# Selective scan on one core: the product with C as one GpSimd instruction for three channel tiles, last columns by DMA, and the diagonal form of B for every state

## The chip, the core and the metric

The kernel runs on one core of one Trainium2 chip. The time is the device time of one launch in microseconds (us). The kernel before was timed in three runs; their median counts. The profile is one execution recorded by the hardware profiler. Its engines are TensorE (PE; its weight loads are listed apart as PEld), VectorE (DVE), ScalarE (ACT), GpSimd (POOL), and SyncE (SP), which here issues most DMA transfers.

## The reference, cut to what matters

The program is a chain of four layers on an image of 8 x 64 x 64 positions and 192 channels. The second layer holds a selective scan over 384 channels, in four directions over the 4096 positions, with 16 states for each channel. Cut down, it computes:

```python
# B = 8 images, K = 4 directions, Din = 384 channels, N = 16 states, L = 4096 positions
x_dbl = einsum('bkdl,kcd->bkcl', xs, x_proj_weight)
dts, Bs, Cs = split(x_dbl, [12, 12 + 16], axis=2)
dts = einsum('bkrl,kdr->bkdl', dts, dt_projs_weight)
A = -exp(A_logs).reshape(4, Din, N)
delta = softplus(dts + dt_projs_bias[None, :, :, None])
for l in range(L):                      # lax.scan
    dA  = exp(delta[l][..., None] * A)
    dBu = delta[l][..., None] * Bs[l][:, :, None, :] * xs[l][..., None]
    h   = dA * h + dBu
    y[l] = sum(h * Cs[l][:, :, None, :], axis=-1)
out_y = y + xs * Ds
```

All arithmetic is in fp32. The layers before and after (a state-space block with convolutions and an MLP, a depthwise convolution with layer norm and projection, two depthwise convolutions) are the same in both kernels.

## The kernel before

`layer1_scan` does the scan. The positions are cut into pieces of 512 (`NJ`), so there are 8 images x 4 directions x 8 pieces = 256 entries in `steps`; a *step* is one of them. Within a step the work runs over the 16 states (`N1`) and, for each state, over the three channel tiles of 128 (`DT`): 48 iterations. A *group* `g` is one state of one step, that is three iterations; `j` counts iterations over the whole stage, 12,288 in all. An engine executes its instructions in the order in which the program issues them, because the scan is built inside `every_engine`, which fixes the order of PE, DVE, ACT and POOL. SP's order is the scheduler's.

Iteration `j` of the main loop does, in this order:

- At the first tile of a group, `fetch(g + 2)` asks SP for a transfer of the row of C for that state, broadcast to 128 partitions (`bc`, 128 x 512, line 993).
- `ahead(j + 2)` makes the two inputs of the recurrence two iterations early. ACT computes the decay `dA` = exp(delta x A) (line 1003). PE forms delta x B x u in a PSUM bank `pd` (three banks), in four blocks of 128 x 128. The tile `dut` holds delta x u with positions on partitions, so PE has to turn it and to scale it by B. For even states (`diagonal(g)`) it does both in one true matmul: `dut` is the weight and `bd` is a diagonal matrix that holds B (line 1009). For odd states ACT has scaled `dut` by B beforehand (`sb`, 128 x 384) and PE only transposes it with the identity (line 1011).
- `scale(g + 2, ...)` lets ACT make those factors two groups early, four per group: `bd` from the identity (128 x 128) or `sb` from `dut` (128 x 384), both at line 987.
- `scan(j)` is the recurrence on DVE, one `tensor_tensor_scan` over 512 positions (line 1044). It writes tile `o` of `h` (128 x 3 x 512, two buffers). POOL multiplies that tile with `bc` into `hc` (six buffers, line 1053). After the third tile POOL copies the last column of each tile to `st`, the start of the same state in the next piece (line 1055).
- `behind(j - 2)` adds the 16 states: PE transposes `hc` in four blocks and accumulates them in the PSUM bank `yt` of that channel tile (`add_rows`, line 942).

Once per step a second sequence from `prepare` is threaded between these instructions. It loads the rows of the next piece (`xt`, `dut`), turns them (line 888), makes delta (PE at line 901, three ACT passes at lines 906 to 912, DVE at line 915), turns delta (line 922) and multiplies it into `dut` (DVE, line 928). `take` copies the finished `yt` out (ACT, line 957), and the copy goes to DRAM. In one of four directions, four blocks per tile with a diagonal of D are added to `yt` (also line 942, tile `dD`).

Of the kernel before, what the change touches and what calls it, by code (L numbers as in the profile page):

```python
# [10 lines left out]
AF = mybir.ActivationFunctionType  # L11
ALU = mybir.AluOpType
# [6 lines left out]
DIN = 384  # L19
DP, DT = 128, 3  # L20
NH, HD, NS = 6, 64, 64
N1, R1, K1 = 16, 12, 4
# [3 lines left out]
NJ = 512  # L26
# [3 lines left out]
class Names:  # L30
    n = 0


def mk(pool, shape, tag, **kw):
    Names.n += 1
    return pool.tile(shape, F32, tag=tag, name=f"{tag}_{Names.n}", **kw)
# [46 lines left out]
def every_engine(tc):  # L83
    ET = mybir.EngineType
    return tc.manual_schedule(engines={ET.PE, ET.DVE, ET.Activation, ET.Pool})
# [586 lines left out]
def layers123(ctx: ExitStack, tc, a, dr, x1, mv1, out, cst):  # L672
# [31 lines left out]
    yk = [[mk(dr, [L, DIN], f"y{b}_{k}") for k in range(K1)] for b in range(B)]  # L704
    layer1_in(tc, a, load, w_in, normed, ur, ut, xd, cst)
    layer1_scan(tc, a, load, ur, ut, xd, yk, cst)
    x2 = [mk(dr, [CP, CT, L], f"x2d{b}") for b in range(B)]
    x3 = [mk(dr, [CP, CT, L], f"x3d{b}") for b in range(B)]
# [123 lines left out]
def layer1_scan(ctx: ExitStack, tc, a, load, ur, ut, xd, yk, cst):  # L832

    nc = tc.nc
    ident = cst[0]
# [15 lines left out]
    sp = ctx.enter_context(tc.tile_pool(name="s1", bufs=2))  # L851
# [87 lines left out]
    def add_rows(yt, src, mat, first, last):  # L939

        for t in range(NB):
            nc.tensor.matmul(  # L942
                yt[:, t * 128 : (t + 1) * 128],
                src[:, t * 128 : (t + 1) * 128],
                mat,
                is_transpose=mat is ident,
                start=first and t == 0,
                stop=last,
                skip_group_check=True,
            )  # L950
# [16 lines left out]


    PER = N1 * DT
    total = len(steps) * PER  # L970
    ready = [{} for _ in steps]
    brows, decay, turned, states, held, outs, sts = {}, {}, {}, {}, {}, {}, {}

    def diagonal(g):
        return g % 2 == 0

    def scale(g, ts):
        if g >= len(steps) * N1:
            return
        m, n = ready[g // N1], g % N1  # L980
        for t in ts:
            if diagonal(g):
                v, src = mk(sp, [128, 128], "bd", bufs=10), ident
            else:
                v, src = mk(sp, [128, DIN], "sb", bufs=8), m["dut"][:, t, :]
            brows[g, t] = v
            nc.scalar.activation(v, src, AF.Copy, scale=m["xt"][:, t, 1 + R1 + n : 2 + R1 + n])  # L987

    def fetch(g):
        if g < len(steps) * N1:  # L990
            bc = held[g] = mk(sp, [128, NJ], "bc", bufs=4)
            n = g % N1
            nc.sync.dma_start(bc, ready[g // N1]["bcd"][n : n + 1, :].to_broadcast((128, NJ)))

    def ahead(j):

        if not 0 <= j < total:
            return
        g, o = divmod(j, DT)
        s, n = divmod(g, N1)  # L1000
        k = steps[s][1]
        dA = decay[j] = mk(sp, [DP, NJ], "dA", bufs=5)
        nc.scalar.activation(dA, ready[s]["dl"][:, o, :], AF.Exp, scale=aneg[:, k, o, n : n + 1])  # L1003
        pd = turned[j] = mk(pb, [128, NJ], "pd")
        cols = slice(o * 128, (o + 1) * 128)
        for t in range(NB):
            dst = pd[:, t * 128 : (t + 1) * 128]
            if diagonal(g):
                nc.tensor.matmul(dst, ready[s]["dut"][:, t, cols], brows[g, t], start=True, stop=True)  # L1009
            else:  # L1010
                nc.tensor.transpose(dst, brows[g, t][:, cols], ident)  # L1011

    def behind(j):
        if not 0 <= j < total:
            return
        g, o = divmod(j, DT)
        s, n = divmod(g, N1)
        b, k, p, _ = steps[s]
        if n == 0:
            outs[s, o] = mk(py, [128, NJ], "yt", bufs=DT)  # L1020
        add_rows(outs[s, o], states.pop(j), ident, n == 0, n == N1 - 1)
        if k == 0 and n == 8:
            add_rows(outs[s, o], ready[s]["u", o], dD[:, o, :], False, False)
        if n == N1 - 1:
            late.append((take, s, o, outs.pop((s, o))))

    def scan(j):
        if not 0 <= j < total:
            return
        g, o = divmod(j, DT)  # L1030
        s, n = divmod(g, N1)
        b, k, p, first = steps[s]
        if k == 0 and n == 5:
            v = ready[s]["u", o] = mk(sp, [DP, NJ], "uD", bufs=DT)
            nc.sync.dma_start(v, ur[b][:, o, p * NJ : (p + 1) * NJ])
        if first and n == 0 and o == 0:
            sts[k] = mk(pp, [DP, DT, N1], "st")
        st = sts[k]
        rev = slice(None, None, -1) if k >= 2 else slice(None)
        last = 0 if k >= 2 else NJ - 1  # L1040
        if o == 0:
            states["h"] = mk(sp, [DP, DT, NJ], "h", bufs=2)
        h = states["h"]
        nc.vector.tensor_tensor_scan(  # L1044
            h[:, o, rev],
            decay.pop(j)[:, rev],
            turned.pop(j)[:, rev],
            0.0 if first else st[:, o, n : n + 1],
            ALU.mult,
            ALU.add,  # L1050
        )
        hc = states[j] = mk(sp, [DP, NJ], "hc", bufs=6)
        nc.gpsimd.tensor_tensor(hc, h[:, o, :], held[g], ALU.mult)  # L1053
        if o == DT - 1:
            nc.gpsimd.tensor_copy(st[:, :, n], h[:, :, last])  # L1055

    with every_engine(tc):
        for _, f, *v in prepare(*steps[0][:3], ready[0]):
            f(*v)
            if f.__name__ == "turned_xd":  # L1060
                tc.keep_in_program_order(nc.scalar.preload_act_table_set("natural_log_exp_and_others"))
        fetch(0)
        fetch(1)
        scale(0, range(NB))
        scale(1, range(NB))
        ahead(0)
        ahead(1)
        todo, late = [], []
        for j in range(total + 3):
            g, o = divmod(j, DT)  # L1070
            s, i = divmod(j, PER)
            if i == 5 and s + 1 < len(steps):
                todo = prepare(*steps[s + 1][:3], ready[s + 1])
            if o == 0:
                fetch(g + 2)
            ahead(j + 2)
            scale(g + 2, ((0, 1), (2,), (3,))[o])
            while late:
                f, *v = late.pop(0)
                f(*v)  # L1080
            scan(j)
            behind(j - 2)
            while todo and todo[0][0] <= i - 5:
                _, f, *v = todo.pop(0)
                f(*v)
# [367 lines left out]
```

## Time and profile before

| | |
|---|---|
| Three runs | 25,094.24, 25,105.1 and 25,116.98 us; median 25,105.1 us |
| Profiled execution | span of 25,098.0 us from the first to the last instruction; the page lists no time around it |
| Busy share of the span | PE 95%, weight loads 74%, DVE 89%, ACT 80%, POOL 70% |
| The scan in the trace | about 6,680 to 22,890 us (first and last product with `bc`), 12,288 products at 1289 ns |
| Scan on DVE | 10,752 at 1262 ns with a start state, 1,536 at 1204 ns without |
| ACT's factors of B | 8,192 `bd` at 395 ns, 8,192 `sb` at 609 ns |
| PE's records | fp32 matmuls leave two records each, transposes one; line 1009: 49,152, line 1011: 24,576, line 942: 49,152 |
| Copies of last columns | 4,096 on POOL at 201 ns |

The page gives the busy time of an engine and, for each group of equal instructions, the count, the busy time and the mean duration of one. Durations on PE include the drain of the pipeline, so they overlap: the distance between starts, not the duration, is what PE's records cost one after the other.

### The profile page before, as it was taken

The numbers are of one execution on the slowest core, as the hardware profiler recorded it, in microseconds if no ns is written. First come the engines' busy times: TensorE is split into PE (matmuls) and PEld (weight loads), VectorE is DVE, ScalarE is ACT, GpSimd is POOL, SyncE is SP. The second block draws the span as 40 slices with busy tenths as digits, with TensorE's granted clock in tenths as the row PEclk, the third lists the DMA queues.
The fourth block names the chain that finished last, engine by engine and source line by source line (L and its number), as shares of the span: only waits on it lengthen the run. The fifth ranks groups of instructions, "written<-read, shape, count | busy, mean of one in ns | idle before, by whom it ended". The sixth has DMA issues, their size and how long they took to land.

```text
span 25098.0 us, 445961 instructions
## 1 busy us (share of the span) xinstructions
PE 23784.2 (95%) x156672; PEld 18458.1 (74%) x156672; DVE 22334.3 (89%) x26682; ACT 20190.7 (80%) x40488; POOL 17651.1 (70%) x18332
## 2 busy tenths in 40 slices
PE   8999999988899999999999999999999999998999
PEld 4444444445688888888888888888888888885333
DVE  6777777766799999999999999999999999998887
ACT  4555555544599999999999999999999999997443
POOL 2322322310399999999999999999999999995110
PEclk8888888899999999999999999999999999999999
DMA  1111111123333333333333333333333333335554
GB/s 59 47 43 46 46 47 43 38 70 114 110 100 95 96 101 95 95 103 95 95 101 97 95 99 98 95 97 100 95 95 104 95 95 102 95 95 157 170 175 122
DMA packets 1506272, 2337.12 MB, mean 93 GB/s; under 512 B 249997, under 2 KB 775949, under 8 KB 1504026
## 3 DMA queue, kind: packets, MB, share of 16 engines
q1 hardware_dynamic: 1496858, 2283.42, 31.5%
q8 instruction: 1236, 20.25, 0.3%
q0 software_dynamic: 7168, 25.17, 0.3%
q14 instruction: 1010, 8.27, 0.1%
HBM read 1847.54 MB, written 460.59 MB: 92 GB/s over the span
## 4 chain that ended last, share of the span: by engine, by line
PE 36%; ACT 31%; DVE 13%; POOL 13%; issue 6%; DMA 0%; POOLq 0%; SPq 0%; DVEq 0%; ACTq 0%
ACT dA L1003 13%; POOL hc L1053 11%; ACT sb L987 7%; PE pd L1009 6%; PE yt L942 5%; DVE h L1044 5%; ACT bd L987 4%; PE cv L1282 4%; PE y L592 3%; PE pd L1011 2%; PE mm L901 2%; PE fc L626 2%; PE y L519 1%; PE cv L774 1%; PE tp L564 1%
## 5 line engine op out<-in xcount | busy, mean ns | idle before, releaser
L1053 POOL TENSOR_TENSOR hc<-h,bc 128x512 f32<-128x512 f32 x12288 | 15431.9, 1289 | 475.6 <-DVE h L1044 341.2
L1044 DVE TENSOR_TENSOR_SCAN h<-dA,st,pd 128x512 f32<-128x512 f32 x10752 | 12949.5, 1262 | 530.1 <-PE pd L1009 374.4
L1003 ACT ACTIVATE dA<-dl,A_logs 128x512 f32<-128x512 f32 x12288 | 8817.1, 718 | 47.0 <-DVE h L1044 39.6
L942 PE MATMUL yt<-sq,hc 128*128 128x128 f32 x49152 | 7489.3, 275 | 200.1 <-POOL hc L1053 93.8
L1009 PE MATMUL pd<-bd,dut 128*128 128x128 f32 x49152 | 6581.4, 277 | 254.4 <-DVE h L1044 232.1
L1009 PEld LDWEIGHTS pd<-bd,dut 128*128 128x128 f32 x49152 | 5968.5, 192 | 609.9 <-PE yt L942 342.9
L942 PEld LDWEIGHTS yt<-sq,hc 128*128 128x128 f32 x49152 | 5669.7, 141 | 644.3 <-POOL hc L1053 624.4
L987 ACT ACTIVATE sb<-dut,xt 128x384 f32<-128x384 f32 x8192 | 4779.5, 609 | 1.1 <-DVE dut L928 1.0
L1011 PE MATMUL pd<-sq,sb 128*128 128x128 f32 x24576 | 3739.5, 275 | 8.5 <-DVE h L1044 0.4
L1011 PEld LDWEIGHTS pd<-sq,sb 128*128 128x128 f32 x24576 | 2823.6, 141 | 479.1 <-DVE dl L915 380.8
L987 ACT ACTIVATE bd<-sq,xt 128x128 f32<-128x128 f32 x8192 | 3026.3, 395 | 0.0
L1044 DVE TENSOR_TENSOR_SCAN h<-dA,pd 128x512 f32<-128x512 f32 x1536 | 1770.8, 1204 | 117.0 <-PE pd L1009 67.2
L1143 POOL TENSOR_TENSOR yin<-yin,yin 128x1536 f32<-128x1536 f32 x64 | 233.9, 3655 | 1635.1 <-DMA yin<-y 892.5
L1282 PE MATMUL cv<-x,dgi 96*96 96x512 f32 (+1 forms) x2560 | 1175.0, 595 | 9.3 <-ACT x L1271 9.1
L481 POOL TENSOR_TENSOR xdt<-xb,dtv 128x384 f32<-128x384 f32 x256 | 217.1, 848 | 1186.6 <-ACT xb L475 1186.6
L234 DVE SCALAR_TENSOR_TENSOR x<-xs,cpe_w,x 96x504 f32<-96x504 f32 (+1 forms) x1024 | 886.6, 866 | 31.8 <-ACT x L222 21.7
L784 DVE SCALAR_TENSOR_TENSOR u<-xa,conv_w,u 128x504 f32<-128x504 f32 x1152 | 850.1, 743 | 50.5 <-ACT u L776 12.5
L1282 PEld LDWEIGHTS cv<-x,dgi 96*96 96x96 f32 x2560 | 413.0, 164 | 638.2 <-issue 604.5
L901 PE MATMUL mm<-xs,w_dt 13*128 13x512 f32 x1536 | 863.0, 641 | 1.8 <-DVE dl L915 1.0
L1055 POOL COPY st<-h 128x3 f32<-128x3 f32 x4096 | 825.0, 201 | 0.0
L1303 DVE SCALAR_TENSOR_TENSOR y<-x,wi,y 96x504 f32<-96x504 f32 x1024 | 796.0, 796 | 17.7
L626 PE MATMUL fc<-ff,fc_w 128*96 128x512 f32 x1536 | 791.0, 621 | 2.7 <-DVE xo L629 2.7
(263 smaller groups left out, 26186.7 us busy)
## 6 DMA issues: line engine op xcount, KB each, us to landing
bc<-bcd SPq DMA_DIRECT2D x4096, 256.0 KB
yin<-y SPq DMA_DIRECT2D x256, 768.0 KB
csb<-csd SPq DMA_DIRECT2D x256, 384.0 KB
dut<-ut SPq DMA_DIRECT2D x128, 768.0 KB
y<-ys SPq DMA_DIRECT2D x128, 768.0 KB
dut<-ut SPq DMA_DIRECT2D x256, 384.0 KB
y<-ys SPq DMA_DIRECT2D x256, 384.0 KB
xt<-x1d SPq DMA_DIRECT2D x128, 384.0 KB
```

The source lines that it names most:

```text
L234: nc.vector.scalar_tensor_tensor(d[:, :, w0:w1], s[:, dy : dy + R, w0 + dx : w1 + dx], w[:, ct, tap : tap + 1], d[:, :, w0:w1], ALU.mult, ...
L626: nc.tensor.matmul(ps, f2w[:, o, ct * CP : (ct + 1) * CP], ff[:, o, :], start=o == 0, stop=o == 5)
L784: nc.vector.scalar_tensor_tensor(uv[:, o, :, w0:w1], tv[:, o, dy : dy + R, w0 + dx : w1 + dx], cw[:, o, tap : tap + 1], uv[:, o, :, w0:w1] ...
L901: nc.tensor.matmul(ps, w_dt[:, k, o * 128 : (o + 1) * 128], made["xs"][0 : 1 + R1, :], start=True, stop=True)
L942: nc.tensor.matmul(yt[:, t * 128 : (t + 1) * 128], src[:, t * 128 : (t + 1) * 128], mat, is_transpose=mat is ident, start=first and t == 0 ...
L987: nc.scalar.activation(v, src, AF.Copy, scale=m["xt"][:, t, 1 + R1 + n : 2 + R1 + n])
L1003: nc.scalar.activation(dA, ready[s]["dl"][:, o, :], AF.Exp, scale=aneg[:, k, o, n : n + 1])
L1009: nc.tensor.matmul(dst, ready[s]["dut"][:, t, cols], brows[g, t], start=True, stop=True)
L1011: nc.tensor.transpose(dst, brows[g, t][:, cols], ident)
L1044: nc.vector.tensor_tensor_scan(h[:, o, rev], decay.pop(j)[:, rev], turned.pop(j)[:, rev], 0.0 if first else st[:, o, n : n + 1], ALU.mult, ...
L1053: nc.gpsimd.tensor_tensor(hc, h[:, o, :], held[g], ALU.mult)
L1282: nc.tensor.matmul(pv[:, :, w0:w1], dgi[:, ct, j, :], sv[:, dy : dy + R, w0 + dx : w1 + dx], start=j == 0, stop=j == len(TAPS) - 1, skip_g ...
```

## The change

The change has three parts. (1) The product with C is made once per group, for all three channel tiles, by one POOL instruction on 128 x 1536 elements, with `bc` repeated over the tiles by a step of zero. `hc` becomes a tile of 128 x 3 x 512 with three buffers, `h` gets three buffers in place of two, and `behind` runs six iterations after the scan (`LAG`) in place of two. (2) The copy of the last columns from `h` to `st` is taken from POOL; SP issues it as a DMA of 128 x 3 single elements, ahead of the product. (3) Every state uses the diagonal form: ACT makes four `bd` per group (14 buffers), and PE four true matmuls per iteration. `sb` and the transposes of line 1011 are gone. Line numbers after the first edited one are 6 to 7 lower in the changed kernel.

```diff
     PER = N1 * DT
+    LAG = 2 * DT
...
-    def diagonal(g):
-        return g % 2 == 0
-
     def scale(g, ts):
...
         for t in ts:
-            if diagonal(g):
-                v, src = mk(sp, [128, 128], "bd", bufs=10), ident
-            else:
-                v, src = mk(sp, [128, DIN], "sb", bufs=8), m["dut"][:, t, :]
-            brows[g, t] = v
-            nc.scalar.activation(v, src, AF.Copy, scale=m["xt"][:, t, 1 + R1 + n : 2 + R1 + n])
+            v = brows[g, t] = mk(sp, [128, 128], "bd", bufs=14)
+            nc.scalar.activation(v, ident, AF.Copy, scale=m["xt"][:, t, 1 + R1 + n : 2 + R1 + n])
...
-            if diagonal(g):
-                nc.tensor.matmul(dst, ready[s]["dut"][:, t, cols], brows[g, t], start=True, stop=True)
-            else:
-                nc.tensor.transpose(dst, brows[g, t][:, cols], ident)
+            nc.tensor.matmul(dst, ready[s]["dut"][:, t, cols], brows[g, t], start=True, stop=True)
...
-        add_rows(outs[s, o], states.pop(j), ident, n == 0, n == N1 - 1)
+        add_rows(outs[s, o], states[g][:, o, :], ident, n == 0, n == N1 - 1)
+        if o == DT - 1:
+            del states[g]
...
-            states["h"] = mk(sp, [DP, DT, NJ], "h", bufs=2)
+            states["h"] = mk(sp, [DP, DT, NJ], "h", bufs=3)
...
-        hc = states[j] = mk(sp, [DP, NJ], "hc", bufs=6)
-        nc.gpsimd.tensor_tensor(hc, h[:, o, :], held[g], ALU.mult)
         if o == DT - 1:
-            nc.gpsimd.tensor_copy(st[:, :, n], h[:, :, last])
+            nc.sync.dma_start(st[:, :, n], h[:, :, last])
+            hc = states[g] = mk(sp, [DP, DT, NJ], "hc", bufs=3)
+            nc.gpsimd.tensor_tensor(hc, h, held.pop(g).unsqueeze(1).to_broadcast((DP, DT, NJ)), ALU.mult)
...
-        for j in range(total + 3):
+        for j in range(total + LAG + 1):
...
-            behind(j - 2)
+            behind(j - LAG)
```

## The prediction

> **What bounds the kernel now.** I read the slices of the page first, then one stretch inside the scan by engine, then that stretch's groups by line, then PE's order of time. The scan is the stage from 6,680 to 22,890 us; nothing else is edited. I take 8,000 to 20,000 us as its sample. This is the stretch; the columns after the 12,000 us are the busy times of PE, PEld, DVE, ACT and POOL, then the granted clock, the DMA share and GB/s.
>
> ```profile
> ...
> 8000.00:20000.00 12000.00, 11660.32 (x96277) 10626.90 (x96276) 11486.90 (x10422) 11720.86 (x23686) 11707.76 (x12127) 1.00 0.35 98
> ...
> ```
>
> Four engines seem full: PE 97%, ACT 98%, POOL 98%, DVE 96%. For PE this is not its true load, because its records overlap. The groups of the same stretch (count, busy time, mean ns, idle before) give what each engine does:
>
> ```profile
> ...
> L1053 POOL TENSOR_TENSOR hc<-h,bc 128x512 f32<-128x512 f32 x9096 | 11422.1, 1289 | 292.3 <-DVE h L1044 192.5 <-PE yt L942 29.2 <-issue 1.7
> L1044 DVE TENSOR_TENSOR_SCAN h<-dA,st,pd 128x512 f32<-128x512 f32 x7945 | 9568.5, 1262 | 392.1 <-PE pd L1009 276.8 <-PE pd L1011 58.9 <-ACT sb L987 22.6
> ...
> L942 PE MATMUL yt<-sq,hc 128*128 128x128 f32 x36385 | 5543.5, 275 | 145.1 <-POOL hc L1053 66.8
> L1009 PE MATMUL pd<-bd,dut 128*128 128x128 f32 x36384 | 4871.7, 277 | 188.6 <-DVE h L1044 172.1
> ...
> L987 ACT ACTIVATE sb<-dut,xt 128x384 f32<-128x384 f32 x6064 | 3537.5, 609 | 0.0
> L1011 PE MATMUL pd<-sq,sb 128*128 128x128 f32 x18192 | 2768.1, 275 | 5.9
> L987 ACT ACTIVATE bd<-sq,xt 128x128 f32<-128x128 f32 x6065 | 2240.5, 395 | 0.0
> ...
> L901 PE MATMUL mm<-xs,w_dt 13*128 13x512 f32 x1134 | 635.3, 640 | 0.0
> ...
> L922 PE MATMUL mm<-sq,dl 128*128 128x128 f32 x2274 | 372.1, 273 | 0.0
> ...
> L942 PE MATMUL yt<-dD,uD 128*128 128x128 f32 x1152 | 152.2, 275 | 0.0
> ...
> L888 PE MATMUL mm<-sq,xt 128*45 128x128 f32 x756 | 113.4, 273 | 0.0
> ...
> ```
>
> Each step has 192 records of the sum over states (48 iterations, four blocks), so 36,385 records are 189.5 steps and a step lasts 12,000 / 189.5 = 63.32 us. What PE's records cost back to back stands in PEld's order of time (start, length, what, count):
>
> ```profile
> ...
> 10002.00 0.47 PEld L942 LDWEIGHTS yt<-sq,hc 128*128 128x128 f32 x4
> 10002.44 0.47 PEld L1011 LDWEIGHTS pd<-sq,sb 128*128 128x128 f32 x4
> 10002.88 0.47 PEld L942 LDWEIGHTS yt<-sq,hc 128*128 128x128 f32 x4
> 10003.32 0.47 PEld L1011 LDWEIGHTS pd<-sq,sb 128*128 128x128 f32 x4
> 10003.75 0.47 PEld L942 LDWEIGHTS yt<-sq,hc 128*128 128x128 f32 x4
> 10004.39 0.29 PEld L901 LDWEIGHTS mm<-xs,w_dt 13*128 13x128 f32 x2 [0.17 <-issue]
> 10005.44 0.42 PEld L1011 LDWEIGHTS pd<-sq,sb 128*128 128x128 f32 x4 [0.76 <-DVE dl L915]
> 10005.83 0.47 PEld L942 LDWEIGHTS yt<-sq,hc 128*128 128x128 f32 x4
> 10006.26 0.97 PEld L1009 LDWEIGHTS pd<-bd,dut 128*128 128x128 f32 x8
> 10007.15 0.47 PEld L942 LDWEIGHTS yt<-sq,hc 128*128 128x128 f32 x4
> 10007.59 0.97 PEld L1009 LDWEIGHTS pd<-bd,dut 128*128 128x128 f32 x8
> 10008.48 0.47 PEld L942 LDWEIGHTS yt<-sq,hc 128*128 128x128 f32 x4
> 10008.92 0.97 PEld L1009 LDWEIGHTS pd<-bd,dut 128*128 128x128 f32 x8
> ...
> ```
>
> Read the starts. From 10002.00 to 10003.75 sixteen transposes follow each other: 1.75 / 16 = 0.1094 us each. From 10006.26 to 10008.92 lie sixteen records of true matmuls and eight transposes: (2.66 - 8 x 0.1094) / 16 = 0.1116 us each. A block of four costs 0.44 us as transposes and 0.89 us as matmuls, since an fp32 matmul leaves two records. Nothing is waited for in these runs, so this is PE's pace. The two records of line 901 cost 10005.44 - 10004.19 = 1.25 us, less 0.05 that the next four regain: 1.20.
>
> PE's need in the stretch is then 57,607 transposes (36,385 + 18,192 + 2,274 + 756) x 0.1094 = 6,302 us; 36,384 + 1,152 records of line 1009 and of D x 0.1116 = 4,189; 567 pairs of line 901 x 1.20 = 680. The sum is 11,171 us, 93.1%, or 58.95 us per step. Only 4.4 us per step are free. The other engines by busy time: POOL 61.8, ACT 61.9, DVE 60.6 us per step. DVE's own pace is longer than its busy time says: its order of time has four scans in 4.88 us, so 48 x 1.22 + 3 x 0.67 (line 915) + 4 x 0.53 (line 928) = 62.7 us. POOL, ACT and DVE set the pace together, and PE is 4 us behind them.
>
> **The change part by part.**
>
> *Product with C.* Three products of 1289 ns and a copy of 201 ns per group go; one product of 128 x 1536 comes. The nearest row is the tail's sum of two dense tiles of this size on POOL (line 1143), 3655 ns mean. Three separate products, 3867 ns, are the upper bound for a fused one, unless the step of zero in `bc` is slow, for which no row speaks. I take 3.66 us: POOL needs 16 x 3.66 = 58.5 us per step in place of 61.8. The gain is real but only POOL's.
>
> *Diagonal form on ACT.* The chain of waits runs along ACT here and shows starts 0.505 us apart for `sb`, 0.29 for `bd`. 32 of 64 factors per step change: 32 x 0.215 = 6.9 us less, ACT falls from 61.9 to about 55 us.
>
> *Diagonal form on PE.* Half of the blocks of `pd` turn from transposes into matmuls. In the stretch, 18,192 records at 0.1094 (1,990 us) become 36,384 at 0.1116 (4,060 us): 2,070 us more, 10.92 us per step. PE then needs 58.95 + 10.92 = 69.87 us per step. This is 7 us above the next engine, and above today's 63.32. It lies on the path, because the 4.4 us of cover that exist are used up first: 6.55 us per step come through.
>
> The Trainium skill ("TensorE: Matmul & The Clock Gate", section "Back-to-back issue gap") gives about 81 ns for a weight load with a matmul of 128 columns in a sustained stream. By an estimate from that figure the 598 records of 128 columns per step would cost 48 us, 52 with line 901, PE would stay under DVE, and the change would bring time. The trace has 109 to 112 ns here at a granted clock of 1.00, and the measurement decides.
>
> *Clock.* The stretch is granted 1.00 with PE at 93%, and the fully packed runs above have the same, so I price a denser PE at the same clock.
>
> *Last columns by DMA.* SP issues 16 more transfers per step, each waiting for a group's third scan. An issue takes 0.32 us (`bc`) to 0.60 us (`xt`, four rows per partition), so 5 to 10 us of SP's 69.9. Behind it in SP's queue stands the fetch of `bc` for three groups later, wanted nine iterations (13 us) on; the column itself is read 16 groups later. The load on the rings, from the queues' view of the stretch: 34.2% of 16 engines over 12,000 us for 768,960 packets is 85 ns per packet; 384 packets at that price are 2.0 us per ring and group, 33 us per step, on top of 21.7 us (34.2% of 63.32): 78% of 69.9. Between nothing and that, none of it reaches an engine; I take nothing.
>
> The Trainium skill ("DMA: Bandwidth & Descriptors", "Rules for kernel authors") speaks against this part: a strided last dimension becomes one descriptor per element. By it a copy is the 384 packets counted above; no row before shows a 4-byte data transfer.
>
> *LAG and buffers.* PE now sums group g - 2 at iteration 3g. At 1.46 us per iteration, that group's third scan ends about 2.4 us into iteration 3g - 6 (0.89 for its blocks, 0.27 drain, 1.22 scan), its product 3.7 us later, and PE asks 6 x 1.46 + 0.89 = 9.6 us in. 3.5 us are spare, so this wait costs nothing; behind it in PE's queue would stand all later blocks of `pd`, and DVE after them. The four more iterations of lag are paid once, at the end: under 10 us.
>
> **Sum.** 256 steps x 6.55 us = 1,677 us. On the profiled span of 25,098 us this is 26,775; the median of the runs lies 7 us above the span, so 26,782, rounded to 26,780 us.
>
> **Rivals.**
>
> *PE is no limit (faster).* If a true matmul's records can follow closer than 0.1116 us when PE is pressed, POOL's and ACT's relief shows, and DVE sets the pace: 62.7 us, 0.62 x 256 = 160 us less, 24,945 us. The point is 62.7 - (58.95 - 10.50) = 14.25 us for 192 records per step, 0.074 us each. For it: POOL and ACT are the busiest today. Against: thousands of these records stand at the same distance, with no wait shown.
>
> *POOL becomes the bound.* From 69.87 / 16 = 4.37 us per product on, POOL is later than PE; each 0.1 us more costs 410 us. At 4.6 us: 16 x 4.6 = 73.6 us per step, 27,740 us. Against: 3655 ns in the nearest row.
>
> *SP or the rings become the bound.* From (69.87 - 21.7) / 16 / 24 = 0.125 us of a ring per element on, the rings are slower than PE; `bc` then comes late and POOL waits. At 0.2 us: 16 x 4.8 + 21.7 = 98.5 us per step, 34,100 us. Against: the 85 ns include packets of 2 KB.
>
> **How the numbers follow.** The forecast has 0.87, the faster rival 0.05, POOL 0.05, the rings 0.03. Half a per cent on the distances is 0.35 us per step, 90 us: the low end is 26,690. Above, a PE that still idles 1 us per step, under a quarter of today's, gives 27,040: the high end. No case but the first rival ends below 25,105 or near it; 0.2%, 50 us, is about what a measurement of this kernel can tell from no change. Faster 0.04, same 0.01, slower 0.95.
>
> **What would show it.** Right: a step of about 69.9 us, PE's starts without gaps (line 1002 at 8 records in 0.89 us), PEld's idle mostly gone, DVE waiting for `pd`, POOL at about 84% and ACT at 79% in the scan, clock 1.00. Wrong: PE with gaps named after POOL's product or after `bc`, a product over 4.4 us, or records of line 1002 closer than 0.11 us.

## The result, and the profile after

The changed kernel takes 26,824.5 us in the median of four runs (26,815.8 to 26,827.1), the kernel before, with one run more than the three above, 25,110.5 us. The ratio is 1.068, with a 95% interval of 1.067 to 1.070: 1,714 us slower. The forecast was 26,780 us in a range of 26,690 to 27,040. The profiled execution took 26,827.1 us, 1.8 us more than its span of 26,825.3.

The stretch from 8,000 to 20,000 us again, by engine (PE, PEld, DVE, ACT, POOL, clock, DMA share, GB/s):

```profile
...
8000.00:20000.00 12000.00, 12000.00 (x103567) 11525.10 (x103566) 10764.27 (x9437) 9676.15 (x21439) 9499.71 (x2746) 1.00 0.37 89
...
```

PE is busy for all of the 12,000 us. POOL has fallen from 98% to 79%, ACT from 98% to 81%, DVE from 96% to 90%. The clock is 1.00 as before. The groups of this stretch by line:

```profile
...
L1048 POOL TENSOR_TENSOR hc<-h,bc 128x1536 f32<-128x1536 f32 x2746 | 9502.2, 3460 | 2500.5 <-DVE h L1037 2453.1 <-POOL hc L1048 36.9
L1037 DVE TENSOR_TENSOR_SCAN h<-dA,st,pd 128x512 f32<-128x512 f32 x7229 | 8979.8, 1272 | 766.5 <-PE pd L1002 354.2 <-ACT dA L997 144.1 <-ACT bd L981 15.0
L1002 PE MATMUL pd<-bd,dut 128*128 128x128 f32 x65888 | 8755.0, 276 | 0.0
...
L942 PE MATMUL yt<-sq,hc 128*128 128x128 f32 x32944 | 4942.2, 273 | 0.0
L981 ACT ACTIVATE bd<-sq,xt 128x128 f32<-128x128 f32 x10978 | 4013.3, 390 | 0.0
...
L901 PE MATMUL mm<-xs,w_dt 13*128 13x512 f32 x1026 | 574.8, 640 | 0.0
...
L922 PE MATMUL mm<-sq,dl 128*128 128x128 f32 x2061 | 337.3, 273 | 0.0
...
L942 PE MATMUL yt<-dD,uD 128*128 128x128 f32 x960 | 126.8, 275 | 0.0
...
L888 PE MATMUL mm<-sq,xt 128*45 128x128 f32 x688 | 103.2, 273 | 0.0
...
```

32,944 records of the sum over states, at 192 per step, are 171.6 steps, so a step lasts 69.94 us, where it was 63.32. Line 1002 has twice as many records as line 942, in every step. With the distances from before, PE's need is 35,693 transposes (32,944 + 2,061 + 688) x 0.1094 + 66,848 x 0.1116 + 513 x 1.20 = 11,981 us of 12,000: nothing is left. PE waits for nothing ahead of lines 1002 and 942. PEld's order of time shows how dense it is:

```profile
...
10003.90 0.47 PEld L942 LDWEIGHTS yt<-sq,hc 128*128 128x128 f32 x4
10004.54 0.29 PEld L901 LDWEIGHTS mm<-xs,w_dt 13*128 13x128 f32 x2 [0.17 <-issue]
10005.59 0.97 PEld L1002 LDWEIGHTS pd<-bd,dut 128*128 128x128 f32 x8 [0.76 <-issue]
10006.48 0.47 PEld L942 LDWEIGHTS yt<-sq,hc 128*128 128x128 f32 x4
10006.92 0.97 PEld L1002 LDWEIGHTS pd<-bd,dut 128*128 128x128 f32 x8
10007.81 0.47 PEld L942 LDWEIGHTS yt<-sq,hc 128*128 128x128 f32 x4
10008.25 0.97 PEld L1002 LDWEIGHTS pd<-bd,dut 128*128 128x128 f32 x8
...
```

Eight records of line 1002 and four of line 942 make 1.33 us, again and again. The gaps listed at lines 901 and 1002 are no waits for others: around the two 512-wide matmuls of line 901 the weight loads pause by the same 0.76 us in both kernels, and PE itself is busy all the time. From the end of the four transposes ahead (10003.90 + 0.44) to 10005.59 the two cost 1.25 us, where the sum has 1.20. The list of waits (who waited for whom, us in total, times, longest) turns over with it:

```profile
...
POOL hc L1048 <- DVE h L1037: 2453.1, 2534, 3.5
ACT dA L997 <- DVE h L1037: 711.6, 942, 1.8
...
DVE h L1037 <- PE pd L1002: 434.7, 656, 1.3
...
PEld pd L1002 <- DVE dl L915: 243.5, 321, 0.8
...
DVE h L1037 <- DMA st<-h: 0.7, 3, 0.2
...
```

Everybody waits for PE, directly or through DVE: POOL for the third scan of a group, ACT for a free `dA`, DVE for `pd`. PE's sum no longer waits for POOL's product. DVE waits 0.7 us in 12,000 for the columns that come by DMA.

### The profile page after: what moved, and what is told of

Same layout as the page of the kernel before. It is cut to its first block, busy times and chain, and to the rows that moved or that the text cites. A ratio compares the mean times of both kernels' runs of the same rounds, so it can differ in the third digit from the quotient of the medians.

```text
span 26825.3 us, 482942 instructions
## 1 busy us (share of the span) xinstructions
PE 25972.0 (97%) x181248; PEld 21323.2 (79%) x181248; DVE 22880.3 (85%) x26682; ACT 18795.0 (70%) x40488; POOL 15999.7 (60%) x6044
## 4 chain that ended last, share of the span: by engine, by line
PE 88%; DVE 7%; ACT 3%; POOL 1%; issue 1%; DMA 0%; SPq 0%; ACTq 0%; DVEq 0%; POOLq 0%
PE pd L1002 41%; PE yt L942 21%; PE cv L1275 4%; PE mm L901 3%; PE y L592 2%; PE fc L626 2%; PE y L519 1%; PE mm L922 1%; PE cv L774 1%; PE tp L564 1%; DVE x L234 1%; DVE u L784 1%; PE mm L342 1%; PE mm L1176 1%; DVE xs L234 1%; PE mm L1194 1%
## 5 line engine op out<-in xcount | busy, mean ns | idle before, releaser
L1048 POOL TENSOR_TENSOR hc<-h,bc 128x1536 f32<-128x1536 f32 x4096 | 14173.0, 3460 | 3821.8 <-DVE h L1037 3750.7
L1037 DVE TENSOR_TENSOR_SCAN h<-dA,st,pd 128x512 f32<-128x512 f32 x10752 | 13357.6, 1272 | 1142.9 <-PE pd L1002 527.4
L1002 PE MATMUL pd<-bd,dut 128*128 128x128 f32 x98304 | 13063.1, 276 | 0.0
L1002 PEld LDWEIGHTS pd<-bd,dut 128*128 128x128 f32 x98304 | 11942.3, 192 | 580.7 <-DVE dl L915 362.6
L981 ACT ACTIVATE bd<-sq,xt 128x128 f32<-128x128 f32 x16384 | 5988.9, 390 | 0.0
L942 PEld LDWEIGHTS yt<-sq,hc 128*128 128x128 f32 x49152 | 5789.6, 142 | 2.6 <-POOL hc L1048 2.6
L957 ACT COPY ys<-yt 128x512 f32<-128x512 f32 x768 | 443.5, 577 | 867.0 <-PE yt L942 867.0
L906 ACT ACTIVATE e<-mm 128x512 f32<-128x512 f32 x768 | 458.5, 597 | 815.7 <-PE mm L901 815.7
L928 DVE TENSOR_TENSOR dut<-mm,dut 128x384 f32<-128x384 f32 x1024 | 571.0, 558 | 501.8 <-PE mm L922 501.7
L234 DVE SCALAR_TENSOR_TENSOR xs<-x0h,cpe_w,xs 96x504 f32<-96x504 f32 (+1 forms) x1024 | 752.5, 740 | 23.7 <-ACT xs L222 2.5
```

The source lines that it names most:

```text
L234: nc.vector.scalar_tensor_tensor(d[:, :, w0:w1], s[:, dy : dy + R, w0 + dx : w1 + dx], w[:, ct, tap : tap + 1], d[:, :, w0:w1], ALU.mult, ...
L942: nc.tensor.matmul(yt[:, t * 128 : (t + 1) * 128], src[:, t * 128 : (t + 1) * 128], mat, is_transpose=mat is ident, start=first and t == 0 ...
L981: nc.scalar.activation(v, ident, AF.Copy, scale=m["xt"][:, t, 1 + R1 + n : 2 + R1 + n])
L1037: nc.vector.tensor_tensor_scan(h[:, o, rev], decay.pop(j)[:, rev], turned.pop(j)[:, rev], 0.0 if first else st[:, o, n : n + 1], ALU.mult, ...
L1048: nc.gpsimd.tensor_tensor(hc, h, held.pop(g).unsqueeze(1).to_broadcast((DP, DT, NJ)), ALU.mult)
```

## The experiments

Two theories were put against each other. Theory A: PE's additional records are the whole loss, because PE had only 4.4 us per step to spare. Theory B: the fused product, the DMA or the lag take part of it. A third question came up on the way: what a version with half of the states diagonal gains from. All twelve runs were timed beside the kernel before (medians of 25,100 to 25,107 us); the times are medians. *The chain* below is what the profile finds when it goes back from the last instruction of the stretch from 8,000 to 20,000 us, each time to what released it; its shares say which engine the time lies on.

### One part alone, and one part undone

```diff
 # e2_diag_only: the kernel before
     def diagonal(g):
-        return g % 2 == 0
+        return True            # "bd" with bufs=14
```

> The kernel before with one edit: every state uses the diagonal form. The product with C stays three instructions, the copy of the last columns stays on POOL, the lag stays two iterations. Theory A (PE's 10.9 us more per step are the whole loss): PE needs 69.9 us per step again, POOL 61.8 and DVE 62.7 hide beside it, so 26,820 us, within 60 us of the changed kernel, and PE's starts without gaps. Theory B (the fused product, the DMA or the longer lag take part of the loss, and the saturated PE is a companion): clearly below the changed kernel, 25,100 to 26,500 us.

Measured: 26,825 us, ratio 1.0685 (1.067 to 1.070). The diagonal form alone gives the changed kernel's time to within a microsecond. Its stretch by engine:

```profile
...
8000.00:20000.00 12000.00, 12000.00 (x103567) 11525.10 (x103566) 10770.19 (x9438) 9645.91 (x21449) 10673.32 (x10982) 1.00 0.31 88
...
```

PE's row is the same as after, to the record, and in both the whole chain lies on PE. POOL, with three products and the copy, is at 89% and still hidden.

```diff
 # e1_half: the changed kernel
     def diagonal(g):
+        return g % 2 == 0      # scale() and ahead() as before, bd bufs=10, sb bufs=8
```

> The changed kernel with one part undone: the diagonal form only for even states, as before; the fused product, the DMA of the last columns, the lag of six and three buffers of h stay. Theory A: PE falls to 58.95 us per step, POOL to 16 x 3.46 = 55.4 us, ACT stays at 61.9, DVE sets the pace with 62.7 us where the kernel before needs 63.32: 24,950 us, 24,880 to 25,050. Theory B: the fused product or the DMA cost time of their own, so it stays above 25,110 us, up to 26,800.

Measured: 24,802 us, ratio 0.988 (0.9865 to 0.989). With the diagonal form undone the rest of the change is not a loss but a gain of 304 us. This is more than the 160 us that I had worked out, so DVE's 62.7 us were too many: the step lasts 62.04 us here. ACT is busy for 11,935 of 12,000 us, and some 60% of the chain lies on it: it is the next bound.

```diff
 # e4_three: the changed kernel
-            nc.gpsimd.tensor_tensor(hc, h, held.pop(g).unsqueeze(1).to_broadcast((DP, DT, NJ)), ALU.mult)
+            for q in range(DT):
+                nc.gpsimd.tensor_tensor(hc[:, q, :], h[:, q, :], held[g], ALU.mult)
```

> The changed kernel with the product with C in three instructions of 128 x 512 per group (issued after the third scan, into the same tile); DMA of the last columns, lag and diagonal form in every state stay. Theory A: POOL then works 16 x 3.78 = 60.5 us of 69.9 per step in place of 55.4, still hidden: 26,820 us, within 30 us of the changed kernel. Theory B (the fused product is part of the loss): faster than the changed kernel by more than 100 us.

Measured: 26,819 us, ratio 1.068. The fused product is worth nothing while PE is full. POOL was busy for 10,297 us of the 12,000 us with three products per group and for 9,500 us with one.

### PE's load taken away elsewhere

```diff
 # e6_fewer_sums: the changed kernel
-        add_rows(outs[s, o], states[g][:, o, :], ident, n == 0, n == N1 - 1)
+        if n % 2 == 0 or n == N1 - 1:
+            add_rows(outs[s, o], states[g][:, o, :], ident, n == 0, n == N1 - 1)
```

> The changed kernel with PE work left out elsewhere: the sum over states on PE leaves out the odd states except the last (7 of 16), so 84 transposes of 0.1094 us per step, 9.2 us, are gone, and the output lacks those states. Diagonal form, fused product, DMA and lag stay. Theory A (any PE work counts in full until the next engine): PE falls to 60.7 us, DVE with 62.7 us per step sets the pace: 24,980 us, 24,900 to 25,150. Rival (the true matmul of the diagonal form is late by its own chain, dut to pd to scan, not by PE's load): within 200 us of 26,820 us.

Measured: 24,941 us, ratio 0.993 (0.992 to 0.995). With 84 transposes per step fewer, every state still in diagonal form, the whole loss is gone. So it is PE's load that counts, not the chain from `dut` through the matmul to the scan. The time is as expected, but not because DVE sets the pace: PE, which needs 60.7 us, is busy for 11,941 of 12,000 us in steps of 62.65 us, and some 87% of the chain still lies on it. Its work is uneven here, more in states that are summed than in those that are not. That this is why it can't use the rest of the step is argued, not shown.

### The share of diagonal states

```diff
 # e3_none: the changed kernel, as e1_half but
+        return False           # sb bufs=12
```

> The changed kernel with no state in diagonal form: all 16 are scaled by ACT (128 x 384) and transposed; fused product, DMA, lag of six stay. From the half-diagonal version ACT gains 32 factors x 0.215 = 6.9 us per step, 61.9 + 6.9 = 68.8, and PE falls to 58.95 - 10.9 = 48.0. Theory A (the share of diagonal states moves work between ACT and PE, and the busier of the two sets the pace): 68.8 us per step, 26,550 us, 26,400 to 26,700. Rival (the transposed form is the better one throughout, so that less diagonal is always faster): under 24,800 us.

Measured: 26,388 us, ratio 1.051 (1.0495 to 1.053); the step lasts 68.3 us. The stretch by engine:

```profile
...
8000.00:20000.00 12000.00, 10001.43 (x72351) 7835.62 (x72349) 10818.73 (x9664) 12000.00 (x21961) 9733.05 (x2811) 1.00 0.38 90
...
```

ACT takes PE's place: 12,000 of 12,000 us. With 0, 8 and 16 states diagonal the kernel takes 26,388, 24,802 and 26,825 us. The form of B moves work between ACT and PE, and both ends overload one.

```diff
 # e7_nine: the changed kernel, as e1_half but
+        return g % 16 in (0, 2, 4, 6, 8, 10, 12, 14, 15)
```

> The changed kernel with 9 of 16 states in diagonal form (states 0, 2, ..., 14 and 15), the others transposed. From the half-diagonal version, each state that is turned to the diagonal form adds 12 blocks x (2 x 0.1116 - 0.1094) = 1.36 us per step to PE and takes 4 x 0.215 = 0.86 us from ACT. PE 58.95 + 1.36 = 60.3 us, ACT 61.7 - 0.86 = 60.8 us, DVE's scans at 1.17 to 1.20 us with its other work 60.3 to 61.7 us. Theory A with ACT as the next bound: 61.2 us per step, 24,590 us, 24,520 to 24,760. Rival (DVE is already the bound at half): within 50 us of 24,802 us or slower.

Measured: 24,897 us, ratio 0.992 (0.9905 to 0.9935): 95 us slower than half. The rival was nearer, but not for its reason: see the last run.

### Where the gain of the half-diagonal version comes from

```diff
 # e9_before_dma: the kernel before
-            nc.gpsimd.tensor_copy(st[:, :, n], h[:, :, last])
+            nc.sync.dma_start(st[:, :, n], h[:, :, last])
```

> The kernel before with one edit: the last columns go by DMA from SP in place of the copy on POOL; three products per group, half of the states diagonal, lag of two. Question: what brings the 300 us of the half-diagonal version. Theory P (POOL's relief: ACT, 61.9 us per step, is next): POOL falls from 61.8 to 16 x 3.78 = 60.5 us, ACT sets the pace, so most of the gain is here: 24,800 to 24,950 us. Theory L (the longer lag and the third buffer of h bring it, by taking waits of PE for the product): within 60 us of 25,107 us.

Measured: 25,393 us, ratio 1.012 (1.010 to 1.013). Neither theory had the DMA by itself lose 292 us. The list of waits names it:

```profile
...
DVE h L1044 <- DMA st<-h: 201.4, 204, 3.1
...
```

By the program, with two buffers of `h`, the first scan of a group writes the buffer that the transfer of two groups earlier has read, and may not start before that transfer has landed.

```diff
 # e12_dma_three_h: the kernel before, as e9_before_dma, and
-            states["h"] = mk(sp, [DP, DT, NJ], "h", bufs=2)
+            states["h"] = mk(sp, [DP, DT, NJ], "h", bufs=3)
```

> The kernel before with the last columns by DMA and, other than in the first run of that edit, three buffers of h in place of two. The first run lost 292 us, and DVE's scans waited there for the landing of the columns (201 us in 12,000 us, up to 3.1 us each). Theory H (the loss is the buffer of h, held until the column has landed): the waits for the DMA go, POOL works 60.5 us in place of 61.8, the waits of PE for the product stay as a lag of two has them: 24,950 to 25,110 us, no slower than the kernel before. Rival (the 384 single elements per group crowd the rings or SP, whatever the buffers): still over 25,300 us.

Measured: 24,936 us, ratio 0.993 (0.992 to 0.995). The third buffer takes the loss away, DVE's waits for the DMA are gone, and the rings were not crowded. The DMA needs this buffer; the change brings both. The third buffer without the DMA was not run, so how much of the 170 us below the kernel before each of the two brings stays open.

```diff
 # e10_lag: the kernel before
-            behind(j - 2)
+            behind(j - 6)       # loop to total + 7, hc bufs=10
```

> The kernel before with the lag of the sum over states raised from two to six iterations and ten buffers of hc in place of six; nothing else. Theory P: POOL still needs 61.8 us and ACT 61.9 us per step, so at most the waits of PE for the product go, which lie in PE's 4 us of slack: within 80 us of 25,107 us. Theory L: 24,800 to 24,900 us.

Measured: 24,750 us, ratio 0.986 (0.9845 to 0.9875), the best with the next run. Theory P falls: the lag alone, with POOL's work unchanged, gains more than the half-diagonal version. In the kernel before PE's sum waited for the product, with two iterations between them:

```profile
...
PEld yt L942 <- POOL hc L1053: 456.7, 1328, 0.5
DVE h L1044 <- PE pd L1009: 327.7, 443, 1.3
...
```

With six iterations the first wait is gone, and the stretch shows ACT and POOL both full:

```profile
...
8000.00:20000.00 12000.00, 11772.32 (x98478) 10902.63 (x98476) 11723.80 (x10665) 11955.64 (x24235) 11923.50 (x12410) 1.00 0.35 100
...
```

ACT 99.6% and POOL 99.4%, at 61.9 us per step; some 65% of the chain lies on ACT, where it was 42% in the kernel before. Before, no engine was truly full: waits cost 1.4 us of each step. The run shows that the longer lag, with the four more buffers of `hc` that it needs, takes them away. That PE's wait for POOL's product passed on to DVE and from there back to POOL is read from the lists of waits.

```diff
 # e8_half_pool_copy: the changed kernel, as e1_half, and
-            nc.sync.dma_start(st[:, :, n], h[:, :, last])
+            nc.gpsimd.tensor_copy(st[:, :, n], h[:, :, last])
```

> The half-diagonal version with the copy of the last columns back on POOL, ahead of the fused product; lag six, three buffers of h. POOL needs 16 x (3.46 + 0.20) = 58.6 us per step, still under ACT's 61.9. Theory P: 24,800 us, within 40 us of the half-diagonal version, so that the DMA adds nothing once the product is fused. Rival: the copy in front of each product delays the sum or the next start: over 24,900 us.

Measured: 24,746 us, ratio 0.986 (0.984 to 0.9875). The copy on POOL is 56 us better than the DMA here, a little outside the 40 us expected, and equal to the lag alone. So once the lag is there, neither the fused product nor the DMA adds anything: ACT is the bound. In the half-diagonal version with the DMA, DVE still waited 16.5 us of the 12,000 us for columns to land, up to 2.1 us each; this is part of the 56 us, and the rest is open.

```diff
 # e13_lag3: the changed kernel
-    LAG = 2 * DT
+    LAG = DT
```

> The changed kernel with the lag of the sum over states cut from six iterations to three. By the prediction's timing the product of a group is done 0.89 + 0.27 + 1.22 + 3.46 = 5.9 us after the start of the iteration of its first tile, and PE asks for it 3 x 1.46 + 0.89 = 5.3 us in, so PE waits, where at six iterations it had 3.5 us to spare. The wait delays the next blocks of pd and the next scan; worked through, the group lasts about 4.67 us in place of 4.37, 4.8 us more per step: 28,050 us, 27,300 to 28,900. Rival (the timing step is too pessimistic, three iterations are enough): within 60 us of 26,820 us.

Measured: 29,214 us, ratio 1.1635. Direction right, size too small, and above the range: 79.3 us per step, 4.6 us above what I had worked out. PEld's order of time shows the wait and what stands behind it:

```profile
...
10007.01 0.97 PEld L1002 LDWEIGHTS pd<-bd,dut 128*128 128x128 f32 x8
10009.22 0.42 PEld L942 LDWEIGHTS yt<-sq,hc 128*128 128x128 f32 x4 [1.24 <-POOL hc L1048]
...
```

PE stops for 1.24 us ahead of the first sum of a group, and the next blocks of `pd` start late. A fused product needs the longer lag.

```diff
 # e11_lag_nine: the kernel before, as e10_lag, and
-        return g % 2 == 0
+        return g % 16 in (0, 2, 3, 5, 7, 9, 11, 13, 15)   # bd bufs=12
```

> A version meant to beat both: the kernel before with the lag of six (24,750 us by itself, ACT busy 99.6% and POOL 99.4% of the scan) and 9 of 16 states in diagonal form, chosen so that no three follow each other (states 0, 2, 3, 5, 7, 9, 11, 13 and 15). ACT loses 0.86 us of 61.9 per step, PE gains 1.36 us to 60.3, POOL keeps 61.8. Theory: POOL is as full as ACT, so little comes: 24,700 us, 24,620 to 24,780. Rival (PE's denser stretches delay the scans, as with the nine states of the earlier run): 24,800 to 24,950 us.

Measured: 24,969 us, ratio 0.994 (0.993 to 0.996), 219 us slower than the lag alone. The list of waits of this run:

```profile
...
ACT ys L957 <- PE yt L942: 269.0, 192, 1.9
...
DVE h L1044 <- ACT dA L1003: 192.1, 602, 0.5
...
```

Once per step ACT stands ahead of the copy of the finished `yt` until PE has delivered it, 1.4 us each time (269.0 / 192; with the lag alone 29.1 us in all), and the decays queued behind that copy come late to DVE. The earlier run with nine states has the same wait, 256.5 us. About 58% of the chain lies on PE here, against about a quarter with the lag alone, though PE needs only 60.3 us of steps of 62.75 us. PE's lateness reaches DVE through ACT's queue before PE is full. That moving the copy would cure it was not tried, so this reading is argued from the waits. Both runs with nine states also have states 15 and 0 in diagonal form, which follow each other where `yt` is finished; a ninth state elsewhere was not tried, so the place may count and not the number.

## Why the prediction was right

**PE's need** was the step that carried it, and it held: 69.87 us per step forecast, 69.94 measured. The distances 0.1094 and 0.1116 us held under full load: eight and four records make 1.33 us by them, and 1.33 us was measured. The whole stage, from PE's first to its last record of the sum, went from 16,209 to 17,908 us, 1,699 more, against 1,677 in the sum. The rest of the difference to 1,714 lies outside the scan or in the scatter of runs, and I have not separated it.

**The cover.** That only 4.4 of 63.3 us per step were free on PE, where its busy share of 97% left no way to see it and the sum of durations even less, was the reading that decided. That this is the mechanism, and not only the number, is shown twice: the diagonal form alone reproduces the time, and PE's load removed elsewhere gives it back.

**The rival "PE is no limit"** asked for records under 0.074 us apart. None came. The 81 ns per pair of the Trainium skill ("TensorE: Matmul & The Clock Gate", "Back-to-back issue gap") do not hold for these fp32 records: with PE wholly busy at clock 1.00 they stand 0.109 to 0.112 us apart.

**POOL** was sized at 3.66 us per fused product and measured 3.46, within its bounds and without effect; so it was busy for 79% in place of the 84% expected, and ACT for 81% in place of 79%. The 3.66 was the mean of a row of 64 with some very long ones (up to 5455 ns); its median, 3437 ns, would have been the better price. **The rings** were bounded by 2.0 us per copy; the measured cost is about 0.25 us (3.9 us per step, shared by 16 copies). In the queues' view, packets per group rose from 253.7 to 652.8 (768,960 / 3,031 and 1,792,708 / 2,746), and the busy share of the rings from 34.2% of 63.32 us to 36.6% of 69.94, that is 21.7 to 25.6 us per step. The Trainium skill's rule of one descriptor per element ("DMA: Bandwidth & Descriptors", "Rules for kernel authors") agrees: 399 more packets per group, of which 384 are the elements. An issue on SP took 0.61 us.

**The lag** cost nothing, as forecast, and PE's wait for the product vanished; a lag of three shows that it was needed.

**What was wrong beside it.** DVE's 62.7 us per step were too many: I divided the length of four scans by four, but it holds the last one in full, and the next instruction starts before that has ended. DVE's order of time in the kernel before has:

```profile
...
10020.77 3.61 DVE L1044 TENSOR_TENSOR_SCAN h<-dA,st,pd 128x512 f32<-128x512 f32 x3
10024.30 0.53 DVE L928 TENSOR_TENSOR dut<-mm,dut 128x384 f32<-128x384 f32 x1
...
```

Three scans take 3.53 us from start to start, 1.18 us each, so DVE needs 48 x 1.18 + 4.1 = 60.7 us. Hence the rival's price of 24,945 us was too high: with DVE at 60.7 us it would be about 24,440 us, an estimate (63.32 - 60.7 us less in each of 256 steps). No run has the changed kernel with a PE that is no limit. And "POOL, ACT and DVE set the pace together" missed the chain through PE's wait for the product, which a longer lag alone removes. Neither touched the forecast, because PE's 69.9 lies above all of them.

## What to carry to other kernels

Cost a busy engine by the distance of its starts in a run without waits, not by busy share or mean duration, and add up its need per step; the difference to the step's length is the only cover there is. Moving work between two nearly full engines is a balance: here 8 of 16 states was the best share tried, and both extremes lost over 1,200 us against the kernel before. When several engines stand at 98%, look for an in-order wait between them before making any of them faster: four more iterations of lag, with four more buffers, gained 350 us with no work removed.

## What the runs showed of the hardware

- A data element of 4 bytes in a DMA costs little of the rings' time: 3.9 us per step more for 399 more packets on each of 16 rings (16 groups x 399 / 16), about 10 ns each, where the mean packet before took 85 ns. Against the run with the diagonal form alone, whose step is as long (30.3% of the rings), it is 4.4 us and 11 ns. The landing is what cost, where a buffer waited for it: with two buffers of `h` the kernel took 25,393 us, with three 24,936.
- A GpSimd product of 128 x 1536 with one operand repeated by a step of zero took 3460 ns. Three of 128 x 512 kept POOL busy for 3750 ns per group in the same place (10,297 us for 2,746 groups), so the gain is 8%; 3 x 1289 ns overstates it, because their records overlap. The dense sum of the same size in the tail takes 3437 ns in the median, so the repeated operand cost next to nothing.
- TensorE was busy for 12,000 of 12,000 us at a granted clock of 1.00.
